# Softplus terms summed in PSUM, an extra link in the side work, and side work between product and scan

## The chip, the cores and the metric

The kernel runs on one core of a Trainium2 chip. A core has five engines with a queue of instructions each: PE (TensorE, matmuls into PSUM), DVE (VectorE), ACT (ScalarE), POOL (GpSimd) and SP (SyncE, which here only issues DMAs). Each engine takes its instructions in program order; semaphores hold an instruction back until its inputs are there. The metric is the device time of one execution in microseconds (us).

## The reference

The input is 4 images of 64x64 tokens with 96 channels. Four layers follow each other. Each adds a mixer of the normalised tokens, and then a feed-forward block (96 to 384 to 96) whose operands are rounded to 8-bit floats. Layer 0's mixer is a gated recurrence over the tokens. The mixers of layers 1 to 3 are two-dimensional selective scans, and nearly all of the time goes there:

```python
dts = einsum("bkrl,kdr->bkdl", dts, dt_w)            # K=4 orders, 192 channels, L=4096 steps
delta = softplus(dts + dt_b)
A = -exp(A_logs)                                     # 192 x N, N=16 states
# per step l:   h = exp(delta_l * A) * h + (delta_l * u_l) * B_l ;   y_l = sum_n h_n * C_l,n
y = y1 + flip(y2) + transpose(y3) + transpose(flip(y4))   # rows, columns, both directions
y = layernorm(y) * silu(z);   out = y @ out_proj.T
```

B, C and dts come from a projection of u (x_proj), and u is the normalised input after a projection, a 3x3 depthwise convolution and SiLU.

## The kernel before, in words

**Stages and tiles.** Layers 1 to 3 times 4 images give 12 stages. The function `scans` (line 855) goes through them one after another. A stage has 24 items: 2 directions, 4 segments of 1024 steps, and 3 chunks of 128 rows, where a row is one channel in one order (rows or columns of the image). An item has 16 tiles, one for each state n. So there are 12 x 24 x 16 = 4608 tiles of 128 x 1024.

**One tile.** `b_rows` (PE, 2 matmuls) spreads B over 128 partitions into a PSUM tile `bc`, of which there are 2. `decays` (ACT) makes `da` = exp(delta*A). `c_rows` (SP) loads C, spread over partitions, by two DMAs. On DVE, `scan` multiplies `bc` by `du` (the product) and runs the recurrence over 1024 steps (the scan, into `h`, 4 buffers). `carry` (ACT) copies the last column of `h`, `times_c` (POOL) multiplies `h` by `c` in place, and `accumulate` (PE, 4 matmuls, which the trace shows as 8) sums over n into the PSUM tile `acc`.

**The main loop** (lines 986 to 1033) writes the engines' order out by hand. Iteration k issues, in this order: carry(k-1); c_rows(k+2), decays(k+2); b_rows(k+1); scan(k); times_c(k-1); after the last tile of an item `store`; then the side work; then accumulate(k-2). With the first tile of a scan (12 stages x 2 directions x 3 chunks = 72 tiles) `scan` also makes POOL zero a `carry` tile. A wrapper (`InOrder`, line 70) keeps each engine's instructions in the order in which the Python code issues them.

**Side work** is written as generators. Each `yield` ends a step; `yield True` says that the next step needs one of two free PSUM banks, and without one the step is put off. Four kinds run:

- `prepare_chunk` (line 806), one step per tile: delta and du for the next item. PE multiplies `dt_proj`; softplus is max(x,0) + log(1+e) with e = exp(-|x|), plus a correction for what rounding 1+e loses; ACT makes the terms, and POOL adds them in three instructions of 128x1024, and multiplies by u in a fourth.
- `prepare_segment` (line 758), one step per tile: B, C and dts of the next segment. It holds the DVE subtraction `rows` between ACT copies.
- a `Job` (line 703): what lies between two stages of one image: `join_orders`, `mixer_out` and `feed_forward` for the layer that ended, `take_in` and `convolve` for the next, strip by strip (8 strips of 512 tokens). A job earns 1.4 steps per tile (1.9 in the last two stages, where the images that are through layer 3 are finished), saves up at most 2, and each step pumps every chain of the job once.
- `logarithms` (line 245): the Ln of all norms that wait for it, in one go, so that ACT changes its table of functions once. It runs inside `prepare_chunk`, and in iteration n == 11.

After the last tile, what is left of the jobs is issued alone; then one more job finishes the last image. Before the first tile, layer 0 (`gated`) runs with the job for image 0 beside its last tiles, and the rest of that job follows alone.

Of the kernel before, what the change touches and what calls it, by code (L numbers as in the profile page):

```python
# [20 lines left out]
C = 96  # L21
NS = 16
DI = 192
R = 6
# [10 lines left out]


CHUNKS = (((0, 0), (64, 1)), ((0, 1), (64, 0)), ((128, 0), (128, 1)))
# [3 lines left out]
NC3 = 48  # L41
XPW = NB3 + 2 * R + NC3
# [59 lines left out]
def metaformer(ctx: ExitStack, tc: tile.TileContext, x, l0_ab, l0_rest, ssm, ffn, out):  # L102
# [58 lines left out]
    stacked = const("stacked", [128, 64])  # L161
    dve.tensor_copy(stacked[0:64], ident[0:64, 0:64])
    dve.tensor_copy(stacked[64:128], ident[64:128, 64:128])
    twice = const("twice", [128, 128])
    dve.tensor_copy(twice[:, 0:64], stacked)
    dve.tensor_copy(twice[:, 64:128], stacked)
# [5 lines left out]
    sel = const("sel", [NB3, NS, 192], BF16)  # L172
    for n in range(NS):
        for k in range(3):
            at = NS * (k % 2) + n
            dve.tensor_copy(
                sel[:, n, 64 * k : 64 * k + 64], mod32[:, at : at + 1].to_broadcast([NB3, 64])
            )
# [7 lines left out]
    minus = const("minus", [128, 1])  # L186
    pool.memset(minus, -1.0)
# [21 lines left out]
    def moments(src, width):  # L209

        st = sb(5, "st", [128, G, 6])
        mv = sb(5, "mv", [128, G, 2])
        for g in range(G):
            dve.bn_stats(st[:, g, :], src[:, g, 0:width])
        for g in range(G):
            dve.bn_aggr(mv[:, g, :], st[:, g, :])
        return mv

    class Norm:
# [7 lines left out]
        def measure(self, src, width, e):  # L227

            mv = moments(src, width)
# [88 lines left out]
    def join_orders(im, s, hold):  # L318
# [26 lines left out]
        for pair in range(2):  # L345
# [7 lines left out]
            yield pair == 0  # L353
        norm = Norm()
# [3 lines left out]
    def mixer_out(im, layer, s, hold):  # L358
# [6 lines left out]
        normalise(yt, yt, DI, norm.r, norm.nm)  # L365
        yield True
        g = []
        for i, (a, b, z) in enumerate(((0, 128, zl), (128, 192, zh))):
# [12 lines left out]
            for v, z, m in ((g[0], zl, 128), (g[1], zh, 64)):  # L381
                pool.tensor_tensor(v[0:m], v[0:m], z[0:m], ALU.mult)
                yield m == 64
        ps = bank("out_proj")
        for q in range(G):
# [4 lines left out]
            yield  # L390
        x1 = sb(2, "x1", [128, G, C])
# [12 lines left out]
    def load_y(im, s, hold):  # L404
# [4 lines left out]
        sp.dma_start(out=yr[64:128], in_=im.y[1, 64:128, t])  # L409
# [18 lines left out]
    def feed_forward(im, layer, s, hold, dst):  # L428
# [6 lines left out]
        normalise(xh, x1, C, norm.r, norm.nm)  # L435
        yield True
        ps = bank("ff_xt")
        transpose_strip(ps, xh, 0, C)
        yield
# [18 lines left out]
        pool.tensor_copy(hq[:, 2, :], late, saturate=False)  # L458
        yield True
# [16 lines left out]
        for g in range(G):  # L476
            pool.tensor_tensor(y[:, g, :], y[:, g, :], b[:, 3 : 3 + C], ALU.add)
        yield
        x2 = sb(1, "x2", [128, G, C])
        pool.tensor_tensor(x2, x1, y, ALU.add)  # L480
        yield
        sp.dma_start(out=tokens(dst, s), in_=x2)
        if layer < 3:
            norm = hold["norm", s] = Norm()
# [75 lines left out]
    def convolve(im, layer, s, hold):  # L560
# [28 lines left out]
        sp.dma_start(out=im.u[1, 64:128, t], in_=raw[0][64:128])  # L589
# [12 lines left out]
        if s == NSTRIP - 1:  # L602
            yield
            sp.dma_start(out=im.u[1, 0:64, :], in_=cols_a[0:64])
# [7 lines left out]
    def between(im, layer, dst=None):  # L612
# [8 lines left out]
        def first():  # L621
            if layer:
                cols_a, part_c = hold["cols"] = columns()
                sp.dma_start(out=cols_a[0:64], in_=im.y[1, 0:64, :])
# [6 lines left out]
                load_y(im, 0, hold)  # L631
            yield
# [70 lines left out]
    class Job:  # L703
# [7 lines left out]
        def step(self):  # L711
            self.credit = min(self.credit + self.rate, 2.0)
# [33 lines left out]
    def load_segment(item):  # L746
# [8 lines left out]
        sg.cs = dram.tile([NC3, T], F32, tag="cs", name="cs")  # L755
        return sg

    def prepare_segment(item, sg):
# [38 lines left out]
        for k in range(2):  # L797
# [3 lines left out]
            yield from project(ps, m, m + NC3, k)  # L801
            act.copy(sg.rows[0:NC3, cols], ps[0:NC3])
            release()
        sp.dma_start(out=sg.cs, in_=sg.rows[0:NC3])

    def prepare_chunk(item):
# [7 lines left out]
        e = sb(1, "e", [128, T])  # L814
        delta, du = sb(2, "delta", [128, T]), sb(2, "du", [128, T])
        for k in range(2):
            cols = slice(k * MM, (k + 1) * MM)
            ps = bank("dt_proj")
            pe.matmul(ps, f, sg.rows[NB3 : NB3 + 2 * R, cols], start=True, stop=True)
            yield  # L820
            act.activation(e[:, cols], ps, AF.Abs, bias=bias)
            act.activation(delta[:, cols], ps, AF.Relu, bias=bias)
            release()
            yield k == 0
        act.activation(e, e, AF.Exp, scale=-1.0)
        act.activation(du, e, AF.Ln, bias=ones)
        logarithms()
        yield
# [579 lines left out]
```

## Time and profile before

| | |
|---|---|
| runs | 20133.44, 20149.6, 20164.85 us, median 20149.6 |
| profiled execution, its own time | 20152.58 us |
| its span, first to last instruction | 20150.8 us |
| busy in the span | DVE 17808.5, PE 16417.6, POOL 15531.3, ACT 12295.0 us |
| granted PE clock, mean over the span | 0.817 |

Busy is the time in which an engine executes; waits and idle time are not in it. The share over the whole span is a mean over three parts that are unlike each other: layer 0 (to 1889 us), the 4608 tiles (to 19680 us) and the tail (to 20151 us). In a group of instructions "out<-in" names the tiles written and read; "x" is the count, and behind the bar stand busy time, mean duration of one in ns, and the idle time of the engine just before them, with what ended most of it. Nearly all instructions carry line 80, that of the wrapper, so groups are told apart by tile names. "SPq" is SP's queue, which issues DMAs. The clock of PE is given in shares of full speed.

### The profile page before, as it was taken

How to read it: one execution, taken by the hardware profiler on the slowest of the kernel's cores; microseconds unless marked ns; L12 is line 12 of the kernel's file. 1: busy time of each engine (PE TensorE's matmuls, PEld its weight loads, DVE VectorE, ACT ScalarE, POOL GpSimd, SP SyncE). 2: the span in 40 equal slices, each digit the busy share in tenths (PEclk: the TensorE clock that was granted, in tenths of full speed). 3: DMA queues.
4: the chain of work that ended last, by engine and by line, in shares of the span. 5: the costliest groups of instructions: out<-in, count | busy, mean ns of one | idle time of the engine just before them, and what ended most of it. 6: DMA issues, size and time to landing. Idle time of an engine off the chain costs nothing. (4 is left out here: it accounts for less than half of the span.)

```text
span 20150.8 us, 220842 instructions
## 1 busy us (share of the span) xinstructions
PE 16417.6 (81%) x70656; PEld 4838.3 (24%) x70656; DVE 17808.5 (88%) x13848; ACT 12295.0 (61%) x19373; POOL 15531.3 (77%) x10470
## 2 busy tenths in 40 slices
PE   8998788787888787788788888788788888887776
PEld 3332121121122222222222222222222222222223
DVE  6665999999999998999999999989999999999881
ACT  4444665665665665665665666666666666666553
POOL 3434888888888887888888888878888888878882
PEclk9898796786887797897887887887887887888775
DMA  0002666666666666666666676666676666676661
GB/s 20 16 18 69 165 181 174 166 186 167 168 184 171 164 179 175 166 182 180 167 187 171 167 189 167 169 180 169 170 187 171 168 187 168 170 188 161 172 169 44
DMA packets 1234532, 3148.68 MB, mean 156 GB/s; under 512 B 428049, under 2 KB 428177, under 8 KB 1227217
## 3 DMA queue, kind: packets, MB, share of 16 engines
q1 hardware_dynamic: 1233360, 3134.55, 58.6%
q8 instruction: 554, 9.08, 0.2%
q14 instruction: 618, 5.05, 0.1%
HBM read 2819.18 MB, written 314.57 MB: 156 GB/s over the span
## 5 line engine op out<-in xcount | busy, mean ns | idle before, releaser
L80 POOL TENSOR_TENSOR h<-h,c 128x1024 f32<-128x1024 f32 x4608 | 10834.6, 2358 | 2827.5 <-ACT carry L80 1727.5
L80 DVE TENSOR_TENSOR_SCAN h<-da,carry,bc 128x1024 f32<-128x1024 f32 x4608 | 10814.5, 2347 | 608.7 <-POOL carry L80 10.3
L80 PE MATMUL acc<-h,stacked 64*64 64x512 f32 x36864 | 6179.1, 747 | 498.7 <-POOL h L80 493.8
L80 ACT ACTIVATE da<-delta,decay 128x1024 f32<-128x1024 f32 x4608 | 5280.9, 1147 | 1648.9 <-DVE h L80 1601.8
L80 DVE TENSOR_TENSOR bc<-du,bc 128x1024 f32<-128x1024 f32 x4608 | 5574.5, 1210 | 611.2 <-PE bc L80 586.0
L80 PE MATMUL bc<-bs,sel 96*128 96x512 bf16 x9216 | 3346.9, 451 | 2071.8 <-DVE h L80 2054.6
L80 ACT COPY carry<-h 128x1 f32<-128x1 f32 x3456 | 649.0, 188 | 3533.7 <-DVE h L80 3529.1
L80 PEld LDWEIGHTS <-sel 96*128 96x128 bf16 x9216 | 551.3, 101 | 6988.6 <-DVE h L80 5085.7
L80 PEld LDWEIGHTS acc<-h,stacked 64*64 64x64 f32 x36864 | 1132.5, 153 | 3286.5 <-issue 1699.7
L80 ACT ACT_TABLE_LOAD x1133 | 1453.6, 1283 | 41.6 <-DVE mv L80 22.5
L80 POOL TENSOR_TENSOR c<-h,c 128x512 f32<-128x512 f32 x384 | 485.7, 1265 | 970.5 <-ACT c L80 614.8
L80 PE MATMUL conv<-pad,tap_lo 128*128 128x512 f32 x1728 | 917.5, 630 | 0.0
L80 PE MATMUL dt_proj<-rows,w 12*128 12x512 f32 x1152 | 828.0, 805 | 0.0
L80 ACT ACTIVATE du<-e,ones 128x1024 f32<-128x1024 f32 x576 | 660.8, 1147 | 228.8 <-POOL delta L80 223.2
L80 PE MATMUL x_proj_b<-u,xp 128*108 128x512 f32 x1152 | 671.9, 699 | 94.3 <-DMA xp<-in_ssm 59.0
L80 ACT ACTIVATE c<-c,l_bias 128x512 f32<-128x512 f32 x384 | 263.5, 686 | 753.0 <-PE c L80 737.9
L80 POOL TENSOR_TENSOR delta<-delta,du 128x1024 f32<-128x1024 f32 x288 | 679.5, 2359 | 12.1 <-ACT du L80 12.1
L80 POOL TENSOR_TENSOR e<-e,du 128x1024 f32<-128x1024 f32 x288 | 679.4, 2359 | 2.4 <-ACT du L80 2.4
L80 POOL TENSOR_TENSOR du<-delta,u 128x1024 f32<-128x1024 f32 x288 | 679.4, 2359 | 0.7
L80 POOL TENSOR_TENSOR delta<-delta,e 128x1024 f32<-128x1024 f32 x288 | 678.5, 2356 | 0.1
L80 PE MATMUL x_proj_c<-u,xp 128*48 128x512 f32 x1152 | 624.3, 655 | 64.3 <-ACT rows L80 64.3
L80 PE MATMUL conv<-pad,tap_hi 128*128 128x512 f32 (+1 forms) x1152 | 638.5, 650 | 8.2 <-ACT u L80 8.2
(155 smaller groups left out, 16118.3 us busy)
## 6 DMA issues: line engine op xcount, KB each, us to landing
c<-cs SPq DMA_DIRECT2D x9216, 256.0 KB, 4.1
u<-u SPq DMA_DIRECT2D x288, 512.0 KB, 7.6
y<-y SPq DMA_DIRECT2D x1152, 128.0 KB, 2.4
y<-y SPq DMA_DIRECT2D x144, 512.0 KB, 5.6
xr<-x SPq DMA_DIRECT2D x224, 192.0 KB, 4.8
u<-u SPq DMA_DIRECT2D x288, 128.0 KB, 4.4
pad<-y SPq DMA_DIRECT2D x288, 128.0 KB, 4.6
z<-zl SPq DMA_DIRECT2D x96, 256.0 KB, 2.0
```

The costliest lines, as they stand in the source:

```text
L80: ins = f(*a, **k).ins
```

## The change

Six things change.

1. `prepare_chunk` works half by half (512 columns). ACT makes e, 1-(1+e), log(1+e) and max(x,0); PE adds the four with identity matmuls into a PSUM bank, and ACT copies the sum to `delta`. POOL keeps the product with u alone. The Ln of the norms goes along with both halves; that of n == 11 is gone.
2. `beside()`, the side work of a tile, is issued from within `scan`, between product and scan. `times_c(k-1)` and `store` are issued ahead of `scan(k)`. Chunks get a second step in every fourth tile.
3. More `yield`s between the steps that make something and the steps that use it; `measure` is cut in three.
4. A job earns 1.8 steps per tile (2.6 in the last two stages) and saves up to 3.
5. `feed_forward` adds its bias in one POOL instruction instead of four, and `x2` takes the buffer of `xh`.
6. The second chunk's halves change places, so that C needs 32 rows, not 48, and no offset.

```diff
-CHUNKS = (((0, 0), (64, 1)), ((0, 1), (64, 0)), ((128, 0), (128, 1)))
+CHUNKS = (((0, 0), (64, 1)), ((64, 0), (0, 1)), ((128, 0), (128, 1)))
...
         def measure(self, src, width, e):
-            mv = moments(src, width)
+            st = sb(5, "st", [128, G, 6])
+            mv = sb(5, "mv", [128, G, 2])
+            for g in range(G):
+                dve.bn_stats(st[:, g, :], src[:, g, 0:width])
+                if g % 2:
+                    yield
+            for g in range(G):
+                dve.bn_aggr(mv[:, g, :], st[:, g, :])
             yield
...
@@ feed_forward
         normalise(xh, x1, C, norm.r, norm.nm)
+        yield
         yield True
         ps = bank("ff_xt")
         transpose_strip(ps, xh, 0, C)
+        yield
         yield
...
         pool.tensor_copy(hq[:, 2, :], late, saturate=False)
+        yield
         yield True
         ps = bank("ff_y")
...
-        for g in range(G):
-            pool.tensor_tensor(y[:, g, :], y[:, g, :], b[:, 3 : 3 + C], ALU.add)
-        yield
-        x2 = sb(1, "x2", [128, G, C])
+        pool.tensor_tensor(y, y, b[:, None, 3 : 3 + C].to_broadcast([128, G, C]), ALU.add)
+        yield
+        x2 = sb(1, "xh", [128, G, C])
         pool.tensor_tensor(x2, x1, y, ALU.add)
+        yield
         yield
...
@@ between, first(): after the loads of y
+            yield
             yield
             yield
...
-            self.credit = min(self.credit + self.rate, 2.0)
+            self.credit = min(self.credit + self.rate, 3.0)
...
@@ prepare_chunk
-        e = sb(1, "e", [128, T])
         delta, du = sb(2, "delta", [128, T]), sb(2, "du", [128, T])
         for k in range(2):
             cols = slice(k * MM, (k + 1) * MM)
+            both = sb(1, "e", [128, T])
+            e, rest, log, top = both[:, 0:MM], both[:, MM:T], du[:, cols], delta[:, cols]
             ps = bank("dt_proj")
             pe.matmul(ps, f, sg.rows[NB3 : NB3 + 2 * R, cols], start=True, stop=True)
             yield
-            act.activation(e[:, cols], ps, AF.Abs, bias=bias)
-            act.activation(delta[:, cols], ps, AF.Relu, bias=bias)
+            act.activation(e, ps, AF.Abs, bias=bias)
+            act.activation(top, ps, AF.Relu, bias=bias)
+            release()
+            yield
+            act.activation(e, e, AF.Exp, scale=-1.0)
+            act.activation(log, e, AF.Ln, bias=ones)
+            logarithms()
+            yield
+            act.activation(rest, e, AF.Identity, bias=ones)
+            act.activation(rest, rest, AF.Identity, bias=ones, scale=-1.0)
+            yield True
+            ps = bank("delta")
+            for i, v in enumerate((e, rest, log, top)):
+                pe.matmul(ps, ident, v, start=i == 0, stop=i == 3)
+                if i % 2:
+                    yield
+            act.copy(delta[:, cols], ps)
             release()
             yield k == 0
-        act.activation(e, e, AF.Exp, scale=-1.0)
-        act.activation(du, e, AF.Ln, bias=ones)
-        logarithms()
...
-        pool.tensor_tensor(delta, delta, du, ALU.add)
...
-        act.activation(du, e, AF.Identity, bias=ones)
-        act.activation(du, du, AF.Identity, bias=minus)
...
-        pool.tensor_tensor(e, e, du, ALU.subtract)
...
-        pool.tensor_tensor(delta, delta, e, ALU.add)
...
         pool.tensor_tensor(du, delta, sg.us[item.chunk], ALU.mult)
...
-        def scan(k):
+        def scan(k, beside):
...
             dve.tensor_tensor(b, i.du, b, ALU.mult)
+            beside()
             h = live[k, "h"] = sb(4, "h", [128, T])
...
-                if n == 11:
-                    logarithms()
...
+            def beside():
+                pump(chain)
+                pump(segment)
+                if n % 4 == 1:
+                    pump(chain)
+                if n == 13:
+                    drain(chain, work)
+                    if item.chunk == 2:
+                        drain(segment, work)
+                work()
...
-            if k <= last:
-                scan(k)
             if 0 <= k - 1 <= last:
                 times_c(k - 1)
             if k >= 3 and (k - 3) % NS == NS - 1:
                 store(items[(k - 3) // NS])
             if k <= last:
-                pump(chain)
-                pump(segment)
-                if n == 13:
-                    drain(chain, work)
-                    if item.chunk == 2:
-                        drain(segment, work)
-                work()
+                scan(k, beside)
...
-            jobs[-1].append(Job(between(im, layer - 1), 1.4))
+            jobs[-1].append(Job(between(im, layer - 1), 1.8))
...
-            jobs[-1].append(Job(between(im, 3, im.dst), 1.9))
+            jobs[-1].append(Job(between(im, 3, im.dst), 2.6))
```

Further single `yield`s stand, in `mixer_out`, before the transposes, before `out_proj` and after it, and in `join_orders` before `measure`.

## The prediction

> **What bounds the kernel now.** I read the page first, then the span cut at the ends of layer 0 and of the tiles.
>
> ```profile
> PE 16417.6 (81%) x70656; PEld 4838.3 (24%) x70656; DVE 17808.5 (88%) x13848; ACT 12295.0 (61%) x19373; POOL 15531.3 (77%) x10470
> ...
> L80 POOL TENSOR_TENSOR h<-h,c 128x1024 f32<-128x1024 f32 x4608 | 10834.6, 2358 | 2827.5 <-ACT carry L80 1727.5
> L80 DVE TENSOR_TENSOR_SCAN h<-da,carry,bc 128x1024 f32<-128x1024 f32 x4608 | 10814.5, 2347 | 608.7 <-POOL carry L80 10.3
> ...
> L80 ACT ACT_TABLE_LOAD x1133 | 1453.6, 1283 | 41.6 <-DVE mv L80 22.5
> ...
> L80 POOL TENSOR_TENSOR delta<-delta,du 128x1024 f32<-128x1024 f32 x288 | 679.5, 2359 | 12.1 <-ACT du L80 12.1
> ```
>
> ```profile
> 0.00:1889.00 1889.00, 1700.70 (x4426) 684.67 (x4426) 1210.03 (x1785) 861.85 (x1776) 696.17 (x1216) 0.92 0.09 23
> 1889.00:19680.00 17791.00, 14438.19 (x64886) 3983.54 (x64890) 16550.84 (x11839) 11258.51 (x17218) 14714.12 (x8973) 0.81 0.65 174
> 19680.00:20151.00 471.00, 278.73 (x1348) 170.13 (x1340) 47.64 (x225) 174.68 (x380) 120.97 (x282) 0.51 0.16 39
> ```
>
> Columns of the second view: stretch, length, busy PE, weight load, DVE, ACT, POOL, PE clock, DMA. In layer 0 PE is the busiest engine (90%), in the tail none is: it is a chain of short steps. In the tiles DVE is busy 93%, and the page's idle times say the same: the scan waits for hardly anything but the product before it, while POOL's `h` idles 2828 us, mostly until ACT has copied `carry`. So time is gained or lost in the tiles only where DVE's own sequence gets shorter or longer. DVE's timeline gives the period, its waits in this stretch the rest:
>
> ```profile
> 9004.74 1.21 DVE L80 TENSOR_TENSOR bc<-du,bc 128x1024 f32<-128x1024 f32 x1
> 9006.08 2.35 DVE L80 TENSOR_TENSOR_SCAN h<-da,carry,bc 128x1024 f32<-128x1024 f32 x1
> 9008.34 1.21 DVE L80 TENSOR_TENSOR bc<-du,bc 128x1024 f32<-128x1024 f32 x1
> ```
>
> ```profile
> DVE bc L80 <- PE bc L80: 586.0, 352, 18.0
> DVE xq L80 <- PE ff_xt L80: 24.0, 27, 1.8
> ...
> DVE h L80 <- POOL carry L80: 10.3, 7, 1.6
> ```
>
> And PE's waits there, which say why `bc` comes late, since PE takes `bc`, side work and `acc` in order:
>
> ```profile
> PE acc L80 <- POOL h L80: 493.1, 374, 5.3
> ...
> PE y_t L80 <- DMA pad<-y: 90.5, 11, 19.1
> ```
>
> A tile takes 3.60 us: product 1.21, 0.13 idle, scan 2.35, and the next product starts 0.09 before the scan's end. 4608 x 3.60 = 16589 of 17791 us; about 600 is DVE's side work, 630 stalls, mostly waits for `bc`. I followed each stall over 0.2 us back to the first engine other than PE: POOL (`h`, `hq`, `u`) 187 us, ACT some 170, DMAs 110, nothing but PE's own work 118.
>
> **The change, part by part** (- is gain). The sum is made against the profiled execution, 20152.6 us, 3.0 above the median.
>
> *Gap hidden, -178.* The scan reads what the product writes, hence 0.13 idle; independent DVE work follows with 0.09 overlap. Side work between the two saves 0.216 per tile that has some. The built order has 826 such tiles (578 tiles had side work before; `measure` is now cut up): 826 x 0.216 = 178. Bounds: 0, if the side work itself waits there for as long as the gap was, and -178. I take the full value: by the built order nearly all of `xq`, `x1` and `st` still stand an iteration or more behind what they read, as before. What is queued behind side work is now the scan, and behind it the next product.
>
> *Zeroing `carry`, +107.* POOL's memset now stands behind `times_c(k-1)`, and the scan behind it waits:
>
> ```profile
> 10733.50 0.11 POOL L80 MEMSET carry<- 128x16 f32 x1
> 10734.81 2.35 POOL L80 TENSOR_TENSOR h<-h,c 128x1024 f32<-128x1024 f32 x1 [1.20 <-ACT carry L80]
> ```
>
> The scan there started at 10735.76. Behind the product that ends at 10737.16 the memset ends at 10737.27: 1.5 late. 71 of 72 first tiles have a predecessor: 71 x 1.5 = 107; bounds 90 (where POOL was early) to 180 (POOL one us later).
>
> *Tail, -105.* Rate 2.6 outruns the added steps: the built order leaves 641 matmuls behind the last tile, not 878. What is left begins at a place that PE reached at 19798 before, and the old job ended at 19859: 61 us, not 180. The four strips moved forward cost DVE 3.3 each (stats, aggregates, `xq`, sum by their rows, less overlap), 14 in all. Bounds -130 to -60.
>
> *Head, +27.* Layer 0's job keeps 1.4 steps per tile but has more of them; two more strips stay behind. Alone one takes 27 us (its `conv` begin at 1749.8, 1776.8, 1804.7), beside layer 0 some 18 of PE: 2 x 9.5, and 8 for the longer first softplus. Bounds 0 to 60.
>
> *First loads, +36.* `first()` has a step more, but by the built order the first `y_t` matmul comes 3 tiles behind its loads, not 4, in eight stages, and 2, not 3, twice in the last. PE waited 90.5 us in 11 places for these loads; each of ten grows by a tile: 10 x 3.6. Bounds 0 to 50.
>
> *POOL relieved, -120.* Out go 3 x 288 x 2.358 = 2037 us, and 128 x 0.55 = 70 in `ff_y` (4 x 0.368 against about 0.92): 83% to 71% busy in the tiles. Of 187 us of POOL's stalls I take two thirds; bounds 0 and -187.
>
> *PE loaded, +45.* 288 x 8 identity matmuls of 0.94 are 2166 us on PE:
>
> ```profile
> 9016.14 1.88 PE L80 MATMUL conv<-pad,tap_lo 128*128 128x512 f32 x4
> ```
>
> (The trace shows one fp32 matmul as two.) At full clock with bc 0.60 and acc 1.09 a tile's PE work goes from 2.70 to 3.17 of 3.60 us on average, and tiles with more than 3.60 from 577 to 1086. A late PE hurts only when it has used up the tile of slack that two `bc` tiles give, so I take 0.09 us for each of the 509. Bounds: -60 (half of the 118, if a busier PE is granted more clock: 0.92 in the head at 90% busy, 0.81 at 81%, 0.51 in the tail at 59%) and +282 (one in three pays the mean wait for `bc`, 586/352 = 1.66). The Trainium skill, "TensorE: Matmul & The Clock Gate", section "What's actually happening", holds that the clock is halved until some 3.4 us of activity release it; by it alone this term would be near the lower end and the total about 105 lower.
>
> *ACT loaded, `rows` +96.* Per item the softplus goes from 7.2 to about 9.1 us (Abs and Relu 2.69, then two each of Exp 0.60, Ln 0.68, copy 0.57, and four Identity 0.68): 288 x 1.9 = 550; table loads go from 1133 to 1521 in the built order: 388 x 1.283 = 498. ACT rises from 63% to 69%, off the path, but DVE's `rows` waits for two ACT copies of the iteration before, and its place is now 2.35 earlier: 4.85 us after ACT's turn begins, not 7.2. In chunk 1 ACT comes with about 1.6 left over from Exp, Ln and two loads (0.6+0.7+2.6 and 1.34 for carry and `da`, less 3.6), and then needs 1.34+1.38+1.16: 5.5 to 5.9. So about 1.0 at 96 of the 192 places. Bounds 0 to +307 (all 192 by 1.6). Behind a waiting `rows` stands the scan, so DVE loses it all. ACT's other stalls (170) I leave: added steps against a longer queue. Table loads of the n == 11 flush are gone, which is why 576 more for the second Ln come to only 388.
> The skill's "ScalarE: Activation LUTs", section "What ACT_TABLE_LOAD costs", adds a drain of 1.38 us to each load: 388 x 2.66 = 1032 instead of 498, and twice 1.4 more in the queue ahead of `rows`, another 250 us. The trace contradicts it: a load begins 0.02 after the instruction before it and the next ACTIVATE 0.01 after it.
>
> *At nothing.* On SP no DMA is added or moved past another: its C loads wait for POOL's `times_c`, which stands in the same place and comes no later; C is stored with 128 KB instead of 192, 96 times, off the path. Next on POOL behind `times_c` come `store` (ACT and SP) and the side work, as before. ACT's order is the same but for the new steps. `x2` in the buffer of `xh` makes the next strip's normalising on ACT wait for the store of `x2`, which lands 2.3 us after its issue and is issued six steps, three tiles or 11 us, earlier; without that cover it would cost ACT up to 2.3 us, 96 times, off the path. Sixteen constants of 0.18 fewer at the start are 3 us.
>
> Sum: -178 +107 -105 +27 +36 -120 +45 +96 = -92: 20060 us.
>
> **The rivals.**
> *PE late* (slower): the upper end of the PE term, 237 more: 20300. It decides once 177 us more than my 45 is lost there, about one of four of the 509 tiles paying 1.66. For it: PE already causes nine tenths of DVE's waits, and four pairs of identity matmuls may meet `x_proj` and `conv`. Against it: the tile of slack, and a clock that rises with load.
> *ACT late* (slower): the upper end of `rows`, 211 more: 20270.
> *Stalls collapse* (faster): POOL's 187, PE's -60, `rows` 30: 20060 - 67 - 105 - 66 = 19820. For it: POOL was behind in most long waits; against it: ACT is behind nearly as many.
> *The gap stays* (the side work waits for its inputs where it now stands): 20060 + 178 = 20240.
>
> **How the numbers follow.** Forecast 44%, spread 19960 to 20160; PE late 20%, ACT late 12%, collapse 18%, gap stays 6%. 0.2% is 40 us, about what three runs that spread by 31 can tell. Of the forecast's 44, 30 lie below 20109, 11 within 40 us, 3 above; collapse adds 18 below, the slower rivals 3 within and 35 above. So 0.48 faster, 0.14 same, 0.38 slower. The range 19860 to 20320 leaves out half of the collapse and the worst of the late engines.
>
> **What the profile after would show.** Right: product and side work without a gap, 826 times; `h<-POOL carry` about 110 us in 70 waits; POOL near 71% in the tiles; tail near 350 us; `rows` waiting for ACT about 100. Wrong: DVE waits for `bc` well over 650 us, or hundreds of us in `rows`, `xq` or `st`.

## The result and the profile after

The changed kernel took 21287.5 us (median of four runs, 21280.0 to 21306.2), against 20141.5 for the kernel before on the same chip: 1.057 times as long, with a 95% interval of 1.0551 to 1.0588. The prediction, 20060 with a range up to 20320, was wrong by some 1230 us and on the wrong side.

The profiled execution has a span of 21288.4 us, 1137.6 more than before. First its page, the busy times and the groups that answer to those shown of before (columns as there: busy us and mean ns of one, then the idle time before them and what ended most of it):

```profile
PE 17657.9 (83%) x75264; PEld 5606.4 (26%) x75264; DVE 17782.1 (84%) x13832; ACT 13292.2 (62%) x21489; POOL 13531.1 (64%) x9221
...
L78 POOL TENSOR_TENSOR h<-h,c 128x1024 f32<-128x1024 f32 x4608 | 10845.2, 2358 | 5636.7 <-ACT carry L78 3950.1
L78 DVE TENSOR_TENSOR_SCAN h<-da,carry,bc 128x1024 f32<-128x1024 f32 x4608 | 10797.9, 2343 | 617.2 <-POOL carry L78 121.6
L78 DVE TENSOR_TENSOR bc<-du,bc 128x1024 f32<-128x1024 f32 x4608 | 5580.1, 1211 | 1514.2 <-PE bc L78 1471.8
...
L78 ACT ACT_TABLE_LOAD x1521 | 1951.4, 1283 | 47.7 <-DVE mv L78 21.4
...
L78 PE MATMUL delta<-e,ident 128*128 128x512 f32 x2304 | 1342.8, 700 | 489.9 <-ACT e L78 405.1
```

Every engine but DVE is off the bound as before, and DVE has as much work as before (17782 against 17809 us). What has grown is its idle time: the product waits 1514 us. The span cut at the same places as before (stretch, length, busy PE, weight load, DVE, ACT, POOL, PE clock, DMA) says where:

```profile
0.00:1980.70 1980.70, 1724.91 (x4442) 675.51 (x4442) 1207.50 (x1768) 865.27 (x1786) 685.22 (x1188) 0.92 0.08 22
1980.70:20930.70 18950.00, 15727.09 (x69853) 4805.54 (x69853) 16539.09 (x11899) 12292.15 (x19414) 12758.35 (x7854) 0.86 0.63 163
20930.70:21288.40 357.70, 205.87 (x973) 125.40 (x969) 35.52 (x166) 134.79 (x290) 87.52 (x181) 0.50 0.18 42
```

The head is 92 us longer (forecast +27), the tiles 1159 (forecast -14), the tail 114 shorter (forecast -105). So the tiles hold the error. DVE's waits there (who waits, for whom: us in all, times, longest):

```profile
DVE bc L78 <- PE bc L78: 1471.8, 802, 25.5
DVE h L78 <- POOL carry L78: 121.6, 71, 3.5
DVE rows L78 <- ACT bs L78: 86.4, 70, 3.9
DVE xq L78 <- PE ff_xt L78: 79.0, 35, 5.2
DVE st L78 <- DMA xr<-x: 59.9, 20, 8.8
```

The waits for `bc` went from 586 us in 352 places to 1472 in 802, so the sign that the prediction named for its own failure ("well over 650") is there. `bc` is PE's, and what PE itself waited for in the tiles is the next view:

```profile
PE bc L78 <- DVE h L78: 1494.9, 1370, 10.2
PE acc L78 <- ACT y L78: 764.1, 239, 8.2
PE delta L78 <- ACT e L78: 395.1, 141, 5.4
PE acc L78 <- POOL h L78: 130.8, 87, 4.4
PE y_t L78 <- DMA pad<-y: 59.5, 11, 24.2
```

Before, the first of PE's waits (other than for DVE) was `acc <- POOL h`, 493 us; that has shrunk to 131, as POOL's relief should make it. In its place stand two waits for ACT. That for `e` is new, and that for `y` was small:

```profile
PE acc L80 <- ACT y L80: 67.3, 72, 5.0
```

Following each DVE stall over 0.2 us back to the first engine other than PE, as in the prediction: 631 us in 359 stalls of the product lead to ACT's `y` (20 us before) and 380 in 157 to ACT's `e`. The product's stalls that lead to POOL fell from 202 us (187 by the prediction's count) to 99: its `hq` from 77 to 8 and `u` from 40 to 6, but `h` only from 85 to 77.

One such stall in the timeline of the changed kernel (start, duration, instruction, and idle time before it with its releaser), on ACT, PE and DVE in turn:

```profile
8372.24 0.67 ACT L78 ACTIVATE e<-dt_proj,w 128x512 f32<-128x512 f32 x1
8372.81 0.67 ACT L78 ACTIVATE delta<-dt_proj,w 128x512 f32<-128x512 f32 x1
8373.38 0.62 ACT L78 ACTIVATE e<-e 128x512 f32<-128x512 f32 x1
8374.02 1.28 ACT L78 ACT_TABLE_LOAD   x1
8375.32 0.72 ACT L78 ACTIVATE du<-e,ones 128x512 f32<-128x512 f32 x1
...
8376.23 1.28 ACT L78 ACT_TABLE_LOAD   x1
8377.53 1.15 ACT L78 ACTIVATE da<-delta,decay 128x1024 f32<-128x1024 f32 x1
8378.58 0.99 ACT L78 COPY y<-acc 128x1024 f32<-128x1024 f32 x1
```

```profile
8375.27 1.03 PE L78 MATMUL bc<-bs,sel 96*128 96x512 bf16 x2 [0.24 <-DVE h L78]
8379.63 1.98 PE L78 MATMUL acc<-u,skipd 64*64 64x512 f32 x8 [3.33 <-ACT y L78]
8381.39 1.93 PE L78 MATMUL acc<-h,twice 64*64 64x512 f32 x8
8383.25 1.04 PE L78 MATMUL bc<-bs,sel 96*128 96x512 bf16 x2
```

```profile
8380.07 2.35 DVE L78 TENSOR_TENSOR_SCAN h<-da,carry,bc 128x1024 f32<-128x1024 f32 x1
8384.33 1.23 DVE L78 TENSOR_TENSOR bc<-du,bc 128x1024 f32<-128x1024 f32 x1 [1.91 <-PE bc L78]
```

This is the third and fourth tile of an item. The chain of `prepare_chunk`, which is advanced twice in the tile n == 1, puts Abs, Relu, Exp, a table load, Ln and the load back into one turn of ACT. Behind them, in tile n == 2, stands the `store` of the item before, whose copy `y` empties `acc`. There is one `acc`; so the first `accumulate` of the new item waits 3.33 us for it on PE, and behind it, in order, stands the `bc` of the next tile. Before, that turn of ACT held Abs and Relu alone.

### The profile page after: what moved, and what is told of

Same layout as the page of the kernel before. It is cut to its first block, busy times and chain, and to the rows that moved or that the text cites. A ratio compares the mean times of both kernels' runs of the same rounds, so it can differ in the third digit from the quotient of the medians.

```text
span 21288.4 us, 230529 instructions
## 1 busy us (share of the span) xinstructions
PE 17657.9 (83%) x75264; PEld 5606.4 (26%) x75264; DVE 17782.1 (84%) x13832; ACT 13292.2 (62%) x21489; POOL 13531.1 (64%) x9221
## 5 line engine op out<-in xcount | busy, mean ns | idle before, releaser
L78 PE MATMUL acc<-h,twice 64*64 64x512 f32 x36864 | 5772.4, 700 | 133.7 <-POOL h L78 133.3
L78 PE MATMUL bc<-bs,sel 96*128 96x512 bf16 x9216 | 3144.4, 427 | 1501.0 <-DVE h L78 1494.9
L78 PEld LDWEIGHTS acc<-h,twice 64*64 64x64 f32 x36864 | 1090.4, 146 | 3087.6 <-issue 2103.4
L78 PE MATMUL delta<-e,ident 128*128 128x512 f32 x2304 | 1342.8, 700 | 489.9 <-ACT e L78 405.1
L78 ACT ACTIVATE e<-e,ones 128x512 f32<-128x512 f32 x1152 | 826.6, 717 | 18.7
L78 PEld LDWEIGHTS delta<-e,ident 128*128 128x128 f32 x2304 | 491.9, 224 | 1026.1 <-ACT e L78 537.0
L78 PE MATMUL dt_proj<-rows,w 12*128 12x512 f32 x1152 | 759.2, 743 | 0.0
L78 ACT COPY delta<-delta 128x512 f32<-128x512 f32 x576 | 333.7, 579 | 613.8 <-PE delta L78 612.0
L78 PE MATMUL x_proj_b<-u,xp 128*108 128x512 f32 x1152 | 602.8, 634 | 102.9 <-DMA xp<-in_ssm 56.2
L78 PE MATMUL delta<-du,ident 128*128 128x512 f32 x1152 | 627.2, 626 | 0.0
```

Source lines behind the costliest of these rows:

```text
L78: ins = f(*a, **k).ins
```

## The experiments

Theory A: the order on ACT. Its bursts hold up `y` and the softplus terms, PE stops in order, `bc` comes late. Theory B: PE's identity matmuls, 2166 us by the prediction's estimate, are themselves too much. Theory C: the loss lies in the place of the side work. Where nothing else is said, the ratio is to the kernel before, run beside it on the same chip (medians 20125 to 20138), with the 95% interval, and the stalls are those over 0.2 us, followed back.

### One step in n == 1

```diff
-                if n % 4 == 1:
+                if n % 4 == 1 and n > 1:
                     pump(chain)
```

> The second step of `prepare_chunk` in tile n == 1 is left out; the doubled steps of n == 5, 9 and 13 stay. Theory A (the order on ACT: Abs, Relu, Exp, Ln and two table loads of one tile stand ahead of the copy `y`, which frees `acc`; PE, which works in order, stops at the next `acc`, and `bc` comes late): `y` now stands ahead of Exp and Ln, so most of the 631 us that stalls of the product led back to `y` goes: 20650, between 20500 and 20850. Theory B (PE is overloaded by 2166 us of identity matmuls): the matmuls are all there, 21290 within 50. Theory C (side work between product and scan loses the time): 21290 within 50.

Measured: 20971.9 us, ratio 1.0416 (1.0400 to 1.0431), 316 less than the changed kernel. PE's waits in the tiles:

```profile
PE delta L78 <- ACT e L78: 564.6, 253, 4.5
PE acc L78 <- ACT y L78: 168.2, 139, 3.9
```

The wait for `y` fell from 764 to 168, and the stalls led by it from 631 to 74. Theories B and C, which expected no gain, fall as the sole cause. Some 240 of the 557 came back elsewhere: everything in the chain now stands a tile later, and stalls led by `e` rose from 380 to 496.

### One step in n == 1, and one more before the matmuls

```diff
-                if n % 4 == 1:
+                if n % 4 == 1 and n > 1:
...
             act.activation(rest, rest, AF.Identity, bias=ones, scale=-1.0)
+            yield
             yield True
             ps = bank("delta")
```

> The changed kernel with the second step in n == 1 left out, and one more `yield` between the two Identity of `rest` and the identity matmuls. The kernel with the single step alone took 20972, and 496 us of its product stalls led back to `e` and `rest` on ACT. Theory A (the matmuls stand too close behind ACT's burst, and PE, in order, holds `bc`): about three quarters of the 496 go: 20600, between 20500 and 20750. If PE's load alone makes `bc` late there, and ACT's name stands in the chain only because its burst falls in the same tile: 20970 within 50.

Measured: 20569.4, ratio 1.0217 (1.0202 to 1.0233). Another 402 are gone. The product's waits for `bc` are down to 760 us in 544 places, and PE's wait for `e` to 18 us; these are the largest of PE's waits left in the tiles, other than for DVE:

```profile
PE acc L78 <- POOL h L78: 210.4, 168, 4.2
PE acc L78 <- ACT y L78: 156.1, 133, 5.5
PE y_t L78 <- DMA pad<-y: 100.6, 11, 22.1
```

All 2304 identity matmuls are still issued (the trace counts each as two). Two places in the order of the steps were worth 718 of the 1150 us.

### No Ln

```diff
-            act.activation(log, e, AF.Ln, bias=ones)
+            act.activation(log, e, AF.Identity, bias=ones)
```

> The changed kernel with Identity(1 + e) in the place of log(1 + e): the same operations on all engines, less two changes of ACT's table per half (1.28 us each); delta is another one. Theory A: ACT's burst ahead of `y` and of the identity matmuls shrinks by 2.6 us, more than the mean stalls of 1.8 us (`y`, 631 in 359) and 2.4 us (`e`, 380 in 157): 20450, between 20350 and 20700. Theory B (PE's matmuls, all still there): 21290 less at most 100.

Measured: 20726.1, ratio 1.0295 (1.0278 to 1.0312): 561 less than the changed kernel, and 26 outside A's range on the slow side; B allowed a gain of 100 at most. Table loads fell from 1521 to 826, the stalls led by `y` from 631 to 332 and by `e` from 380 to 174. So the length of ACT's burst counts; what is left of it, Abs, Relu, Exp and Identity, still leads 506 us of product stalls.

### Two of the four identity matmuls

```diff
-            act.activation(rest, e, AF.Identity, bias=ones)
+            act.activation(rest, e, AF.Identity, bias=ones, scale=-1.0)
...
-            for i, v in enumerate((e, rest, log, top)):
-                pe.matmul(ps, ident, v, start=i == 0, stop=i == 3)
-                if i % 2:
-                    yield
+            for i, v in enumerate((rest, top)):
+                pe.matmul(ps, ident, v, start=i == 0, stop=i == 1)
+                yield
```

> Two of the four identity matmuls of each half are left out, and delta is max(x,0) + exp(-|x|) instead of softplus; ACT's work is all there, and the last of it (`rest`) is still waited for. PE loses 1083 us of matmuls. Theory A: the waits for ACT stay, less about half a microsecond of matmuls behind each: 21200, between 21000 and 21300. Theory B: half of the 1160 us that the tiles lost: 20700, between 20500 and 20850. Theory C: 21290 within 60.

Measured: 21011.1, ratio 1.0437 (1.0420 to 1.0455), 276 less than the changed kernel. That is A's range, at its fast end, and far from B's. PE's waits for `y` (744 us) and `e` (566, more than the 395 of the changed kernel) are there; what the edit makes shorter is the work that PE must do between the end of such a wait and the next `bc`.

### Softplus on POOL

`prepare_chunk` as before, and in the loop:

```diff
-                if n % 4 == 1:
-                    pump(chain)
...
+                if n == 11:
+                    logarithms()
```

All else is as changed.

> Only the softplus is undone: terms summed by POOL over 1024 columns, one step per tile, Ln of the norms at n == 11 as before; everything else of the change stays. Theories A and B: the loss goes with the softplus; left are the terms of the sum that are not its own (gap -178, zeroing +107, tail -105, first loads +36, the head's measured +92 less some 30 for the softplus): about 20065, between 19950 and 20200. Theory C: the loss stays, 21000 or more.

Measured: 20555.3, ratio 1.0211 (1.0195 to 1.0226). The loss through the softplus is 732 us, as much as its better order had given back: 20569 with all matmuls on PE and two steps moved, 20555 with the sum on POOL. But 418 us of loss are left, where A and B expected a gain of 70, and C a loss of 860 or more: there is a second cause outside the softplus, and a smaller one than C.

### Side work after the scan

```diff
+            if k <= last:
+                scan(k)
             if 0 <= k - 1 <= last:
                 times_c(k - 1)
             if k >= 3 and (k - 3) % NS == NS - 1:
                 store(items[(k - 3) // NS])
             if k <= last:
-                scan(k, beside)
+                beside()
```

> Only the position is undone: `scan`, `times_c`, `store`, side work, `accumulate` in the order of before; the softplus stays on PE. Theories A and B: the loss stays; by the sum the gap (178) comes back and the zeroing of `carry` (107) and `rows` (86) go: 21270, between 21050 and 21500. Theory C: 20300 or less.

Measured: 21098.7, ratio 1.0477 (1.0461 to 1.0493), 189 less than the changed kernel. C, which put all the loss here, falls; A and B expected about 20 less. DVE's waits in the tiles without the new place:

```profile
DVE bc L78 <- PE bc L78: 1471.5, 803, 24.9
...
DVE xq L78 <- PE ff_xt L78: 18.6, 14, 3.0
...
DVE h L78 <- POOL carry L78: 7.7, 5, 3.0
```

The waits of the product are the same to the microsecond. Against this run the changed kernel gains 172 us in DVE's gaps of up to 0.2 us (from +75 to -98 in sum; overlaps count as negative) and loses 368 in longer stalls: the scan 112, `st` 84, `rows` 80, `xq` 60, `x` 32.

### Place alone

The kernel before with the same move:

```diff
             if k + 1 <= last:
                 b_rows(k + 1)
-            if k <= last:
-                scan(k)
             if 0 <= k - 1 <= last:
                 times_c(k - 1)
             if k >= 3 and (k - 3) % NS == NS - 1:
                 store(items[(k - 3) // NS])
             if k <= last:
-                pump(chain)
...
-                work()
+                scan(k, beside)
```

> The kernel before with only the place changed: side work between product and scan, `times_c` and `store` ahead of `scan`. By the terms of the prediction (578 tiles x 0.216 = -125, zeroing +107): 20120 within 60. Theory F (side work waits for its inputs where it now stands, and what waits there holds the scan, so that the 0.216 per tile is given back): 20330, between 20230 and 20450.

Measured: 20301.2, ratio 1.0082 (1.0067 to 1.0097), 165 more than before. Theory F holds. The waits in the tiles:

```profile
DVE bc L80 <- PE bc L80: 472.9, 298, 18.7
DVE xq L80 <- PE ff_xt L80: 157.5, 78, 4.2
DVE h L80 <- POOL carry L80: 130.7, 71, 4.4
DVE st L80 <- POOL x L80: 71.7, 45, 4.0
```

The small gaps gain 129, as the prediction's 0.216 per tile says for the 578 tiles of this kernel (125), and 111 of the waits for `bc` go. In exchange the zeroed `carry` costs 131 (10 before) and side work that waits in its new place some 300: what used to wait beside a running scan now holds it.

### Softplus and place undone; steps and rates stay

The changed kernel with the two edits shown above, softplus on POOL and side work after the scan, together.

> Softplus on POOL and side work after `scan`, both as before; the added steps, the higher rates, the one-instruction bias, the buffer of `x2` and the exchanged halves stay. If the losses add up: 20555 less the 189 that the place of the side work took from the changed kernel: 20365 within 60, of which head +85, tail -110, so that the tiles still lose some 250. If the place only hurts together with the softplus: 20555 within 60.

Measured: 20441.2, ratio 1.0151 (1.0135 to 1.0166), above its range: 305 more than before, with the head at 1971, the tail at 293 (-178) and the tiles at 18175 (+384). So what is left of the change, the added steps and the higher rates above all, costs 305 by itself; the one-instruction bias, the buffer of `x2` and the exchanged halves are in it and were not taken apart. From here, putting back the place costs 114 and then the softplus 732, or the softplus 658 and then the place 189: with the 305, 1151 either way. In the kernel before the place alone cost 165.

### Only the added steps, old rates

```diff
-            self.credit = min(self.credit + self.rate, 3.0)
+            self.credit = min(self.credit + self.rate, 2.0)
...
-            jobs[-1].append(Job(between(im, layer - 1), 1.8))
+            jobs[-1].append(Job(between(im, layer - 1), 1.4))
...
-            jobs[-1].append(Job(between(im, 3, im.dst), 2.6))
+            jobs[-1].append(Job(between(im, 3, im.dst), 1.9))
```

(On top of the run before, softplus and place undone.)

> As the kernel with softplus and place undone, and the rates 1.4 and 1.9 and the cap of 2 as before; the added steps stay. Theory D (higher rates bunch up to three steps of side work in one tile, and the bunch delays `bc`): the tiles come back to 17790 within 60; the tail grows to 500 to 600, since more steps at the old rate leave more behind; total 20250 within 100. Theory E (the added steps themselves, the buffer of `x2` or the exchanged halves cost): the tiles stay at 18000 or more.

Measured: 20498.2, ratio 1.0179 (1.0163 to 1.0194). Neither theory had it: the tiles are at 17975.5, the tail at 518. DVE's timeline shows a place of its own:

```profile
7686.33 2.35 DVE L78 TENSOR_TENSOR_SCAN h<-da,carry,bc 128x1024 f32<-128x1024 f32 x1
7731.02 1.23 DVE L78 TENSOR_TENSOR bc<-du,bc 128x1024 f32<-128x1024 f32 x1 [42.34 <-PE bc L78]
```

Eight stages have such a hole, of 40.7 to 42.3 us, 331 in all. It stands where the next stage's first segment is loaded (item 22, n == 4): the job must have ended by then, and the loop issues what is left of it in one go. By the issued order these are 45 to 53 turns of one or two steps each here, 9 turns in two stages before, and at most 2 in the changed kernel. A cap of 2 also cuts the rate of 1.4 down to four steps in three tiles, and 1.9 to three in two. So the longer chains need a higher rate, or they leave a hole; outside the holes the tiles took 17645, less than the 17791 before.

### Rates of the two ends

```diff
-            self.credit = min(self.credit + self.rate, 2.0)
+            self.credit = min(self.credit + self.rate, 3.0)
...
-        gated(images, Job(between(images[0], 0), patience=1), pl0)
+        gated(images, Job(between(images[0], 0), 2.0, patience=1), pl0)
...
-            jobs[-1].append(Job(between(im, 3, im.dst), 1.9))
+            jobs[-1].append(Job(between(im, 3, im.dst), 2.6))
```

(On the kernel before.)

> The kernel before with 2.6 steps per tile in the last two stages (cap 3) and 2.0 beside layer 0; nothing else. By the terms of the prediction the tail goes from 471 to some 350, and the strips moved beside layer 0 take 10 to 50 from the head, for some 20 more in the tiles: 20010, between 19950 and 20060. Theory D: three steps in one tile delay `bc` in the last two stages, which gives half of the tail's gain back: 20080 or more.

Measured: 20215.1, ratio 1.0035 (1.0021 to 1.0049). The tail is 292, 179 shorter, but the last stage took 94 more and the one before it 27, five of the middle stages some 16 more each (the cap of 3 lets 1.4 be 1.4), and the head is 58 longer although the job had ended with layer 0: moved beside an engine that is 90% busy, the job's steps cost more than they did behind it.

### Rate 2 at the end

```diff
-            jobs[-1].append(Job(between(im, 3, im.dst), 1.9))
+            jobs[-1].append(Job(between(im, 3, im.dst), 2.0))
```

> The kernel before with 2.0 steps per tile instead of 1.9 in the last two stages, where the cap of 2 cuts 1.9 down to 1.5: the jobs then end with the last tile, and nothing is left for the tail but the last image. By the run with 2.6: tail -180, stages 10 and 11 +120 at 2.5 steps, less than that at 2: 20020, between 19980 and 20080. If the steps cost as much beside the tiles as behind them: 20136 within 25.

Measured: 20027.0, ratio 0.9949 (0.9934 to 0.9964). Its three stretches:

```profile
0.00:1891.70 1891.70, 1702.44 (x4426) 684.92 (x4426) 1210.00 (x1785) 862.24 (x1776) 698.24 (x1216) 0.92 0.09 23
1891.70:19728.20 17836.50, 14449.47 (x65366) 4014.26 (x65366) 16566.35 (x11920) 11336.99 (x17379) 14773.97 (x9093) 0.82 0.64 173
19728.20:20028.00 299.80, 179.03 (x872) 109.17 (x864) 30.22 (x144) 103.91 (x227) 70.33 (x161) 0.50 0.18 44
```

The tail gains 171 and the tiles pay 46, since two even steps in each tile just end the jobs. One digit makes the kernel 0.5% faster than before.

### Place, added steps where they are needed, even rates

The kernel before, the new place, and:

```diff
             if 0 <= k - 1 <= last:
                 carry(k - 1)
...
+            if k <= last and n == 0 and item.first:
+                carries[item.chunk] = sb(2, f"carry{item.chunk}", [128, NS])
+                pool.memset(carries[item.chunk], 0.0)
             if 0 <= k - 1 <= last:
                 times_c(k - 1)
```

with one more `yield` before `x1`, `xq` and two of the `measure` (layers 1 to 3), cap 3, and rates 1.45 and 2.2.

> The kernel before with the side work between product and scan, `carry` zeroed ahead of `times_c`, one more step before `x1`, `xq` and two of the `measure`, in layers 1 to 3 only, and rates that just end each job in time (1.45, cap 3; 2.2 in the last two stages); softplus on POOL. From the run with the place alone (20301): zeroing -120, the waits of `xq`, `st` and `x` -200 of 320, the end -100 as with rate 2, the higher rate +50 to +100: 19950, between 19850 and 20080. If the longer steps bunch as they did with the rates of the change: 20250 or more.

Measured: 20057.9, ratio 0.9962 (0.9949 to 0.9975), above the point expected and within the range. The zeroing's wait is gone (all waits of the scan: 30 us, not 147), and `xq`, `st` and `x` fell from 320 to 232. The first three stages, whose jobs carry the images from layer 0 to layer 1 and had no added step in `feed_forward`, were some 18 slower each than before.

### The same, with the added steps there too

```diff
-        if layer:
+        if layer or linked:
             yield
         xq = sb(1, "xq", [C, MM], F8)
...
+    linked.append(True)
     with tc.tile_pool(name="pac", bufs=1, space=bass.MemoryType.PSUM) as pac:
```

and the same condition ahead of the `measure` of `x2`.

> The run with place, links and even rates (20058), with the added steps also in the jobs beside the first three stages, where the waits of `st` and `xq` remained: 20 less in each of the three: 19995, between 19950 and 20060. If the place itself is not worth its waits: 20058 within 25.

Measured: 19965.3, ratio 0.9926 (0.9909 to 0.9942), 93 less than the run before it and at the fast end of the range. So the place between product and scan pays once what stands there has its inputs. How much is not shown alone: the run is 62 below rate 2 at the end (20027), but its rates differ, and no run has these steps and rates behind the scan.

### Softplus on PE, spaced, old place

The kernel before with the changed `prepare_chunk`, both steps apart as above, the Ln of n == 11 left out, and rates that end the jobs without a rest:

```diff
+                if n % 4 == 1 and n > 1:
+                    pump(chain)
...
-            jobs[-1].append(Job(between(im, layer - 1), 1.4))
+            jobs[-1].append(Job(between(im, layer - 1), 1.65))
...
-            jobs[-1].append(Job(between(im, 3, im.dst), 1.9))
+            jobs[-1].append(Job(between(im, 3, im.dst), 2.5))
```

> The kernel before with the softplus summed on PE, its steps spaced (no doubled step in n == 1, one step between `rest` and the matmuls), and rates that just end the jobs (1.65 and 2.5, cap 3); side work after `scan`. To be compared with the run with rate 2 at the end (20027), which has the softplus on POOL. Theory A (only the order on ACT cost): POOL's relief and PE's load about even out, and the higher rate costs some 100: 20130, between 20030 and 20200. Theory B (PE's matmuls themselves cost): 20300 or more.

Measured: 20462.6, ratio 1.0168 (1.0153 to 1.0183): outside A's range, in B's. But the rates are not those of the run with rate 2 (20027), so the next run takes them alone.

### The rates of that run alone

The last two lines of that diff, and the cap of 3, on the kernel before; softplus on POOL.

> The kernel before with the rates 1.65 and 2.5 and the cap of 3, softplus on POOL, nothing else. Theory A (the order and the bunched steps cost, the sum on PE by itself nothing): as much as the spaced softplus on PE, 20420, between 20370 and 20500. Theory B (PE's matmuls cost by themselves): the rates cost about half, 20230, between 20130 and 20300.

Measured: 20392.7, ratio 1.0137 (1.0120 to 1.0154): within A's range. Of the 435 us between PE's sum and the run with rate 2, the rates alone give 365, and PE's sum at the same rates another 70. The waits of the product in the tiles:

```profile
DVE bc L80 <- PE bc L80: 803.3, 437, 21.1
```

against 586.0 in 352 before. The matmuls in the tiles are as many as with rate 2 (65366); the jobs only end sooner (item 16 to 19 of 24, not 19 to 22). That the bunch on PE in tiles with two or three steps makes `bc` late fits this, but no run separates PE's bunch from ACT's and POOL's. PE's sum needs these rates because `dt_proj` and `delta` hold one of two free banks for more tiles, and steps of the job fall out: by the issued order a job takes 558 steps, against 505 at the same rates with the softplus on POOL. So at equal rates the jobs do not end equally late: in the middle stages they end in item 21 with PE's sum and in item 19 without it. In the run "Rates of the two ends", with the softplus on POOL, they also end in item 21, and there most middle stages lose some 16 us against before, with PE's sum some 43. The price of PE's sum by itself thus lies somewhere between 70 and 435 us; no run makes both the rates and the ends equal.

### Both, spaced

As the spaced softplus on PE, with the place, the added steps and 1.6 and 2.6.

> As the run before it, with the side work between product and scan, `carry` zeroed early, the added steps before `x1`, `xq` and two of the `measure`, and 1.6 and 2.6 as rates. If place and softplus add up and the place is worth what the small gaps say (-120, less the waits of side work, some +80): 20090, between 20000 and 20200. If the waits of `rows` and `xq` for the longer ACT queue grow: 20250 or more.

Measured: 20486.0, ratio 1.0180 (1.0165 to 1.0195), 24 more than in the old place; the waits of `rows` (109 us, against 26) and `st` (147, against 34) eat what the gap gives. With the longer queue on ACT the place is worth nothing here (the rates differ a little).

### The best version

On the run at 19965:

```diff
-        for g in range(G):
-            pool.tensor_tensor(y[:, g, :], y[:, g, :], b[:, 3 : 3 + C], ALU.add)
+        pool.tensor_tensor(y, y, b[:, None, 3 : 3 + C].to_broadcast([128, G, C]), ALU.add)
...
-            jobs[-1].append(Job(between(im, layer - 1), 1.45))
+            jobs[-1].append(Job(between(im, layer - 1), 1.45 if layer > 1 else 1.25))
```

> The run with place and links everywhere (19965), with the bias of `feed_forward` in one POOL instruction, and 1.25 steps per tile beside the first three stages, where the jobs had room. POOL has 70 us less work, of which a third may show in `bc`, and less bunching 10 a stage: 19930, between 19890 and 19970.

Measured: 19954.1, ratio 0.9918 (0.9903 to 0.9933), the fastest of all and within its range. The step from the run at 19965 lies within the intervals of both, and the tiles, 17754 us in either, show no gain from the two edits.

Cut at the same places (head to 1902.7, tiles to 19656.7, tail to 19952.2 us), it has against before 176 less in the tail, 36 less in the tiles and 14 more in the head. Of the change it keeps the place, the links that side work on DVE needs and the bias; it leaves the softplus on POOL, zeroes `carry` earlier and sets the rates to what the jobs need.

## Why the prediction was wrong

*Gap hidden (-178): right in size.* Place against no place, all else as changed, moves the small gaps by 172. Its condition, that side work has its inputs, was taken from the order and not from the waits, and failed: beyond zeroing and `rows`, the stalls of `st`, `xq`, `x` and the rest come to some 176 more in the changed kernel, and in the kernel before, with `rows`, to some 300. The rival *gap stays* had named this.

*Zeroing (+107): right*, 112 more in the scan's stalls. *`rows` (+96): right*, 86 in 70 places. *Tail (-105): right*, -114.

*POOL relieved (-120): right in the stalls, not in the time.* Some 100 us of the stalls that POOL led are gone, but DVE shows no gain from them: even with the two steps moved, the kernel (20569) is no faster than with the softplus on POOL (20555).

*First loads (+36): wrong, and small.* PE's waits for `pad` did not grow: 90.5 us before, 59.5 after, in 11 places each.

*Head (+27): wrong by 65.* By the issued order 149 steps of the job, not 102, stand alone behind layer 0. With the softplus on POOL these 47 steps take 82 us (head 1971), 1.76 each, and the 56 of the run with only the added steps 109, 1.95 each; the softplus adds 9. I had counted strips at PE's price; with nothing beside them, the added steps themselves cost.

*PE loaded (+45), the step that failed.* It priced a late PE by PE's own load ("A late PE hurts only when it has used up the tile of slack"), and next to it stands "ACT's other stalls (170) I leave: added steps against a longer queue", and under *At nothing* "ACT's order is the same but for the new steps". The order was the same, and that was the trouble: the new steps and their table loads take ACT 5.3 us in one tile (8372.24 to 8377.53 in the view of ACT above), and behind them in that unchanged order stands `y`, for which PE waits. The rows for this were there: Abs to Ln by their durations, the two table loads that I had counted for `rows` in chunk 1, and `store` in n == 2 behind them. I followed that queue to DVE's `rows` and not to PE's `acc`. The product stalls that lead to `y` and `e` are 631 + 380 us; the term was between -60 and +282. Two moved steps, with every matmul kept, gave 718 us of the time back.

*Rates: no term at all in the tiles.* The rate was priced in the tail alone, and in the tiles only by "The four strips moved forward cost DVE 3.3 each". The same work at 1.65 and 2.5 lost 266 us against before, and 365 against rate 2 at the end. Higher rates and added steps together, with the smaller edits, are 305 of the loss; that the old rates would leave holes of 41 us was not seen either.

The rival *PE late* had the right symptom, late `bc`, and a ceiling of 282 us against 1011, because it multiplied PE's busy tiles by a mean wait. Its threshold is a slip, too: 132 us above the 45 make the forecast 0.2% slower than before, and 177 is the whole term. Theory B, its mechanism, has no sure price: 70 us at equal rates once the steps are spaced, and up to 435 with the rates that PE's sum asked for.

## What to carry to other kernels

Where engines run in order, cost an added instruction by what stands behind it in its queue, engine by engine, until the bound engine is reached: here ACT's burst, `y` behind it, `acc` behind that on PE, and `bc` behind `acc`. Side work that is spread must be spread evenly and must end just in time: faster costs stalls, slower leaves a rest that is issued in one lump. A place that hides a gap on the bound engine is worth it only for work whose inputs are there an iteration earlier.

## What the runs showed of the hardware

A stall of PE can be paid twice, since PE's clock is often at half behind it. The granted clock in the view by stretches, for the 3.3 us in which PE waited for `y` above and the 4.7 us after it (columns as before):

```profile
8376.30:8379.60 3.30, 0.00 (x1) 0.00 (x0) 3.17 (x3) 3.29 (x4) 2.34 (x1) 0.50 0.27 61
8379.60:8384.30 4.70, 4.67 (x19) 1.48 (x20) 2.69 (x2) 4.24 (x9) 2.53 (x2) 0.51 0.69 156
```

The 16 `acc` and two `bc` matmuls behind such a wait took 2.49 us (median) where the wait was 0.3 to 1 us, 3.83 where it was 2 to 3, and 4.42 where it was over 3 (13, 65 and 114 places of the changed kernel). In the stall shown, PE reached the end of `bc` 4.67 us after the wait, against the 2.49 of the short waits: the difference of 2.2 us is more than the product's whole stall of 1.91. Over the 226 places with a wait of over 1 us it comes to some 310 us of PE time.

Not all of that is the wait's own doing. In the stall shown the clock had fallen some 6 us before the wait began: `bc` took 0.60 us, and in the next tile, behind two waits for DVE, 1.04:

```profile
8367.23 0.60 PE L78 MATMUL bc<-bs,sel 96*128 96x512 bf16 x2 [1.10 <-DVE h L78]
...
8371.12 1.04 PE L78 MATMUL bc<-bs,sel 96*128 96x512 bf16 x2 [1.21 <-DVE h L78]
```

Of the 114 waits of over 3 us, 40 began at the half clock and 108 ended at it; of the 65 of 2 to 3 us, 6 and 23. All spells of one clock in the trace last a whole multiple of 3.41 us, which suggests that the cost of a wait also depends on where in such a piece it falls. In the 3.41 us before a fall PE was busy for 42% of the time (median of 654 falls in the tiles).

The prediction had taken the clock for a gain from a busier PE, and the mean did rise, from 0.81 to 0.86 in the tiles; but behind the waits of over 3 us for `y` it is 0.55 on average.

The Trainium skill, "TensorE: Matmul & The Clock Gate", section "What's actually happening", says that the clock is halved again after an idle window of some 3.4 us. The length of the window agrees with the trace; but here shorter waits are enough: 2 us behind their end, 42 of the 65 waits of 2 to 3 us had the half clock.
